# One kernel of cross attention and a state-space scan: block 0's sampled maxima spread on TensorE, a longer planned transfer for the other blocks, and a new table of dates

## The chip, the cores and the metric

The kernel runs on one core of one Trainium2 chip. Its time is the device time of one execution in microseconds (us); three timed runs of the kernel before gave a median of 1900.03 (1899.72 to 1900.69). The core's engines are named as in the profile: PE is TensorE (products), PEld its weight load, DVE VectorE, ACT ScalarE, POOL GpSimd, SP SyncE, which issues most DMA transfers; "ACTq" and "SPq" are the DMA issues in ACT's and SP's streams. Each engine runs its own instructions strictly in the order in which the program gave them.

## The reference

All is float32. 4096 queries (rows of x, 512 wide) attend to 3202 context rows, with 8 heads of 64:

```python
xq, kv = layernorm(x, g1, beta1), layernorm(ctx, g1, beta1)
x = x + mha(xq, kv)                      # softmax over 3202 keys, then W_o, b_o
xn = layernorm(x, g2, beta2)
U = (xn @ W_in.T + b_in) @ Bmat          # 64 wide
s = silu(s @ A.T) + u_t                  # a scan over the 1024 steps of each of 4 rows
out = x + s @ Cmat + (program_probs.mean(1) @ W_prog.T + b_prog)
```

## The kernel before

**Prologue.** `lead()` prepares the context: 26 chunks of at most 128 keys are loaded (cx), normalised (xh), transposed to channel-major ct (on PE, tile tp_c, or by DVE and DMA), and multiplied by the key and value weights wk and wv. Four chunks make a group. Group 0 is multiplied plainly (products pv and pk). Groups 1 to 5 use a scheme with seven products in place of eight (`seventh`, L503: pkx, pky, pvx, pvy); ACT copies the one half of a result (ks, vs), DVE joins the other (L699), and SP stores keys in kd and values in vd. The last group is chunk 24 and a chunk of two keys; the values of these two go through `second` (L728, ACT, and L729, DVE) into the tile vx, by four DMA stores (L734).

**Sample.** The exponents of a block of queries need an offset that is at least near the largest score. For each block of 512 queries, products of its queries with a sample of the keys (sm, L426) are copied by ACT to ex (L442, "held"); DVE takes their maximum m over each partition (L446); the maxima of all partitions have to reach all partitions, and go out to DRAM and come back broadcast (md<-m, L449, "sent"; all<-md, L453, "got", both on SP); DVE reduces these to the offsets `shifts` and to `marks` (L459 to L462, "base"); and ACT turns the sample's scores into weights (L467, "extra"), since two of the sampled columns are keys of the sequence that are in no chunk.

**Attention.** There are 8 blocks of queries, in units of two heads each; for each half chunk of keys, PE makes scores s (L1280), ACT weights p=exp(s) with the offset (L1324), DVE adds them in acc (L1332), and PE multiplies by the values into po (L1386, and L1375 for ex with vx). At the unit's end, ACT copies and DVE joins the two parts of acc (L1355, L1309, L1360) and of po (L1467, L1474). PE runs scores some groups ahead of products. The last block goes in halves; behind it the tail finishes the scan.

**What sets the order.** `Plan.order()` (L153) simulates the engines while the program is built, and appends to each engine, whenever it is free, the ready piece with the earliest due time. A piece has a cost, pieces that it comes after, rings (buffers) that it takes and gives back, and a due time to which `SHIFT[name] * STEP` (STEP is 2150 ns) is added; LATE adds a delay before another engine sees a result (`"SP": 5000` for a transfer). The costs and dates exist only in that simulation: they decide the order of instructions, not how long the chip takes. One plan makes the prologue (with `used(c)` and `start_of(g)` as base dates), another attention and tail. `sample_pieces` adds a block's sample to either.

Of the kernel before, what the change touches and what calls it, by code (L numbers as in the profile page):

```python
# [10 lines left out]
F32 = mybir.dt.float32  # L11
# [9 lines left out]
P = 128  # L21
TB = 32
NC = H // P
NCH = 26
CK = 128
NDC = NCH // 2
REST = S2 - (NCH - 1) * CK
GC = 4
# [48 lines left out]
class Plan:  # L77
# [19 lines left out]
        "a": 31.5, "add": 70, "add.h": 168, "add.l": -0.25, "added": 30.75, "b": 38, "base": 4.75,  # L97
        "close": -10.5, "copied": 80.5, "counted": 21.25, "den": -120, "den.l": -21, "differ": 46.5,
        "extra": -64.75, "fall": 325.25, "fall.h": 51.75, "fall.l": -4.25, "fold.h": -94.5, "fold.l": 17.5,
        "gather": -4, "gather.h": -20, "gather.l": 41.25, "got": 5.75, "held": 14.75, "inverse": 86.5,  # L100
        "inverse.h": -73.5, "inverse.l": 49.5, "join": -20.5, "join.h": -32, "join.l": 82.5, "joined0": 167.5,
        "joined1": 27.5, "l.copy": 36.25, "l.factors": 17, "l.from": 127, "l.h": 7.25, "l.idle": 354.5,
        "l.inputs": 16.75, "l.kept": -25, "l.mod": -54.75, "l.near": -48.25, "l.out": 23.5, "l.scaled": 24.25,
        "l.states": 141, "l.stats": 402.5, "l.terms": 43, "l.turn": 199.5, "l.x1": -10.25, "l.ys": -4.75,
        "l.z": -59.25, "last": 37.75, "maximum": -59.75, "number": 40.75, "open": 0.5, "output": -7.75,
        "output.h": -18.75, "output.l": -43.25, "outs": 1.5, "outs.read": -4.25, "product": -7.25,
        "products": 30, "py1": 17, "query.factors": 4.25, "query.flip": 381.5, "query.load": 1.25,
        "query.move0": -7.5, "query.move1": -39.25, "query.move2": -38, "query.move3": 29.25,
        "query.scaled": 130.75, "query.stats": 673.25, "rest": 5, "rest.h": -59.75, "rest.l": -51,
        "risen": 16, "row.copy": 25.25, "row.flip": 59.5, "row.kept": -28, "row.load": -73.75,  # L110
        "row.mod": -54.75, "row.move0": 78.75, "row.move1": -81.5, "row.move2": 26.75, "row.move3": 146.5,
        "row.scaled": 88, "row.stats": -20.75, "row.store": 190.5, "row.x1": -56, "rows.first": 8.5,
        "rows.inputs": 577.75, "rows.outs": -105.25, "rows.s": 38, "rows.turn": 3.75, "sample": -21.5,
        "scale": -90.5, "scale.h": -17, "scale.l": 4.5, "scores": -8.5, "sevenths": -324.5, "sq": -9.5,
        "start": -45.75, "states": -0.5, "stored0": -22.25, "sums": 5.75, "sums.h": -0.5, "sums.l": -4.25,
        "swap": 65.5, "swap.h": 3.5, "swap.l": -19.25, "table": 18.25, "to": 7.75, "tq": 62.75,
        "weights": 17.75, "yb": -25, "a.load": 176, "bu": 72.25, "c.copy": -73.25, "c.factors": 11,
        "c.flip": 129, "c.load": -50.5, "c.move": -3.75, "c.scaled": -1.25, "c.stats": 4.75, "c.turn": -10.75,
        "d.bi": -16, "d.bm": 249.75, "d.cb2": 54.75, "d.rows": -23.75, "d.win": 17.5, "d.wo": -2,
        "d.wq": -221.25, "d.x0": 18, "h0": -29.5, "in": -84, "in.bi": 1.75, "in.bm": 21.75, "in.cb": -16.25,  # L120
        "in.cb2": 119, "in.rows": -45.5, "in.win": 126, "in.wk": 56, "in.wo": 0.5, "in.wq": -58.25,
        "in.x0": -103.75, "k": 1.25, "k.copy": -57.25, "k.sample": -12, "keep": 2, "marks": -22, "mean": 49,
        "modb": 17.5, "p": 14, "pb": 35, "pm": 49.75, "prm": 257.75, "prr": 69.5, "pt": -50.5, "pw": -26.25,
        "rowb": 64.25, "rowv": -21.5, "rowv.w": 108.75, "s": 33.5, "store": -22.75, "sums_": 2.75,
        "t": 218.25, "tied": 2.75, "v": 123.25, "wct": -62.25, "wk": -19.5, "wk.bias": -1.5, "wk.g": -64.75,
        "wk.pb": -83, "wk.w": -61.5, "wq": 2.75, "wq.bias": -7.75, "wq.g": -6.25, "wq.pb": 56.75,
        "wq.w": 56.5, "wv": 139.25, "wv.bias": 87.25, "wv.pb": 120, "wv.w": 11.75, "x.copy": 4,
        "x.factors": 108.75, "x.scaled": -158.25, "x.turn": 13.5, "heads": 41.5, "q": -13.75,
# [119 lines left out]
def xattn_ssm_kernel(  # L248
# [22 lines left out]
    nc = tc.nc  # L271
# [136 lines left out]
    def sampled_by(Q):  # L408

        v = {}  # L410
# [53 lines left out]
        def extra():  # L464
# [3 lines left out]

        return (
            ("sample", "PE", 870, sample, ["m", "m"], []), ("held", "ACT", 1200, held, ["ex"] if Q else [], ["m"]),  # L470
            ("maximum", "DVE", 1100, maximum, ["max"], []), ("sent", "SP", 300, sent, [], []),
            ("got", "SP", 300, got, [], []), ("base", "DVE", 700, base, [], ["max"]),
            ("extra", "ACT", 1300, extra, [], []),
        )

    def sample_pieces(add, Q, after, d, of_q=()):

        name, before, opened = None, after, {}
        for i, (name, engine, cost, run, takes, gives) in enumerate(sampled_by(Q)):
            for ring in takes:  # L480
                opened[ring] = (name, Q)
# [2368 lines left out]
```

## Time and profile before

| what | value |
|---|---|
| median of three runs | 1900.03 us (1899.72 to 1900.69) |
| profiled execution, its span | 1901.1 us, 1899.3 us |
| mean granted TensorE clock | 0.993 |
| PE busy | 1861.1 us, 98% of the span |
| DVE, ACT, POOL busy | 1492.1 us (79%), 1141.3 us (60%), 305.6 us (16%) |
| PE busy in 0 to 200 us, 200 to 1830, 1830 to the end | 186.16 of 200, 1617.97 of 1630, 56.99 of 69.3 |

In the rows quoted below, a time line's row gives the start and the duration in us, the engine and line, the operation with its result and sources, and in brackets the idle time of the engine just before it and what ended that. "<-issue" means that the profile shows nothing that it waited for. A row of waits gives the total idle time, how often, and the longest. Durations of groups ("x16") run from the first to the last of consecutive like instructions.

### The profile page before, as it was taken

To read this page: it belongs to the slowest core of one execution; us is meant where nothing else is said; L and a number is where in the kernel's file an instruction comes from. 1 tells how busy PE (TensorE), PEld (TensorE's weight loads), DVE (VectorE), ACT (ScalarE), POOL (GpSimd) and SP (SyncE) were. 2 spreads that over 40 slices of the span, in tenths; PEclk is the share of its full clock that TensorE was granted. 3 is DMA by queue.
4 is the path that set the end of the run, shared out by engine and by line. 5 is a ranking of instruction groups with operands and counts; after the bars stand their busy time and mean duration, and the time that the engine had idled before them with its cause. 6 is when DMAs were issued, how large, how long until landed. Compare 5 with 4: busy or idle time off the path is not lost.

```text
span 1899.3 us, 44466 instructions
## 1 busy us (share of the span) xinstructions
PE 1861.1 (98%) x17952; PEld 920.0 (48%) x17952; DVE 1492.1 (79%) x1731; ACT 1141.3 (60%) x1407; POOL 305.6 (16%) x395
## 2 busy tenths in 40 slices
PE   8899999999999999999999999999999999999997
PEld 5788433434343343434343434334443434577674
DVE  6541488789887889688978887888978897888776
ACT  3332377565766657565757576775667575657653
POOL 5220121001210221022101220022102210111105
PEclk9999999999999999999999999999999999999999
DMA  6652322250434124331434043413432143435667
GB/s 230 165 160 83 88 77 70 57 148 29 126 92 126 51 75 126 107 87 39 124 76 135 28 125 89 133 44 99 115 102 80 47 126 89 150 108 153 179 183 240
DMA packets 262993, 207.05 MB, mean 109 GB/s; under 512 B 95918, under 2 KB 236222, under 8 KB 262784
## 3 DMA queue, kind: packets, MB, share of 16 engines
q1 hardware_dynamic: 258764, 197.54, 36.7%
q10 hardware_dynamic: 4020, 6.62, 1.2%
q8 instruction: 143, 2.34, 0.5%
q14 instruction: 66, 0.54, 0.1%
HBM read 157.37 MB, written 29.89 MB: 99 GB/s over the span
## 4 chain that ended last, share of the span: by engine, by line
PE 81%; DMA 3%; DVE 2%; ACT 2%; issue 1%; ACTq 0%; DVEq 0%; SPq 0%; POOLq 0%
PE s L1280 29%; PE po L1386 29%; PE po L1411 5%; PE s L1293 4%; PE qx L503 3%; PE pax L503 3%; PE pay L503 2%; PE qy L503 2%; DMA all<-md 2%; DMA md<-m 1%; ACT p L1324 1%; PE pd L1440 1%; DVE acc L1332 1%; PE pu L1900 1%; PE po L1375 1%
## 5 line engine op out<-in xcount | busy, mean ns | idle before, releaser
L1324 ACT ACTIVATE p<-s,shifts 128x1024 f32<-128x1024 f32 x804 | 888.2, 1109 | 412.1 <-PE s L1280 345.7
L1332 DVE TENSOR_TENSOR acc<-p,acc 128x1024 f32<-128x1024 f32 (+1 forms) x732 | 911.4, 1250 | 115.2 <-ACT p L1324 88.8
L1280 PE MATMUL s<-q,k 64*64 64x512 f32 x5600 | 724.2, 591 | 11.9 <-ACT p L1324 11.9
L1386 PE MATMUL po<-p,v 64*64 64x512 f32 x5600 | 722.3, 590 | 0.0
L1280 PEld LDWEIGHTS s<-q,k 64*64 64x64 f32 x5600 | 211.0, 133 | 401.3 <-issue 355.4
L1386 PEld LDWEIGHTS po<-p,v 64*64 64x64 f32 x5600 | 212.1, 133 | 355.9 <-issue 330.2
L1787 POOL TENSOR_TENSOR xr<-xr,rowb 128x512 f32<-128x512 f32 x28 | 35.4, 1273 | 701.1 <-DVE acc L1332 608.0
L1498 DVE RECIPROCAL rd<-rd 128x256 f32<-128x256 f32 (+1 forms) x64 | 110.2, 1721 | 27.5 <-ACT rd L1493 27.5
L1411 PE MATMUL po<-p,v 64*64 64x256 f32 x1600 | 112.2, 377 | 0.0
L1293 PE MATMUL s<-q,k 64*64 64x256 f32 x1600 | 112.1, 377 | 0.0
L1882 POOL TENSOR_TENSOR xr<-x,modb 128x512 f32<-128x512 f32 x28 | 35.3, 1269 | 279.9 <-DVE x L1835 265.7
L1293 PEld LDWEIGHTS s<-q,k 64*64 64x64 f32 x1600 | 67.3, 133 | 25.5 <-issue 3.8
L1411 PEld LDWEIGHTS po<-p,v 64*64 64x64 f32 x1600 | 67.2, 133 | 21.3 <-issue 1.7
L1568 POOL TENSOR_SCALAR rstd_x<-mv_x 128x1 f32<-128x1 f32 x28 | 30.6, 1093 | 279.5 <-DVE mv_x L1565 277.8
L1576 ACT ACTIVATE xh_y<-x,nm_y,rstd_y 128x512 f32<-128x512 f32 x30 | 24.2, 807 | 83.5 <-POOL nm_y L1570 83.5
L1332 DVE TENSOR_TENSOR acc<-p,p 128x1024 f32<-128x1024 f32 x36 | 44.6, 1239 | 27.5 <-ACT p L1324 27.3
L699 DVE TENSOR_TENSOR ks<-pky,ks 128x512 f32<-128x512 f32 x15 | 10.4, 690 | 49.7 <-PE pky L503 30.7
L1718 ACT ACTIVATE q<-qx,bias 128x256 f32<-128x256 f32 x42 | 17.6, 470 | 50.8 <-PE qx L503 50.8
L693 ACT ACTIVATE ks<-pkx,bias 128x256 f32<-128x256 f32 x40 | 16.7, 469 | 47.9 <-PE pkx L503 34.8
L1360 DVE TENSOR_TENSOR acc<-swap,acc 64x512 f32<-64x512 f32 (+1 forms) x70 | 44.1, 630 | 1.2
L1355 ACT COPY swap<-acc 64x512 f32<-64x512 f32 (+1 forms) x70 | 40.2, 574 | 2.0 <-DVE acc L1339 0.8
L598 DVE STREAM_TRANSPOSE x<-xh_x 128x512 f32<-128x512 f32 x28 | 19.6, 704 | 15.2 <-ACT xh_x L1576 10.7
(319 smaller groups left out, 1750.9 us busy)
## 6 DMA issues: line engine op xcount, KB each, us to landing
k<-kd SPq DMA_DIRECT2D x432, 128.0 KB, 2.6
v<-vd SPq DMA_DIRECT2D x432, 128.0 KB, 2.6
xn<-x SPq DMA_DIRECT2D x448, 32.0 KB, 1.9
xr<-in_x_dram SPq DMA_DIRECT2D x30, 256.0 KB, 4.2
x1d<-xr SPq DMA_DIRECT2D x30, 256.0 KB, 3.1
x<-in_x_dram SPq DMA_DIRECT2D x28, 256.0 KB, 4.0
cx<-in_ctx_dram SPq DMA_DIRECT2D x25, 256.0 KB, 3.8
vd<-vs SPq DMA_DIRECT2D x40, 128.0 KB, 2.1
```

The costliest lines, as they stand in the source:

```text
L503: nc.tensor.matmul(to[:, b, :], still[:, i, b * P : (b + 1) * P], moving[:, i, :], start=(start and b == 0 and i == 0), stop=(i == 1), ski ...
L1280: nc.tensor.matmul(s[k0 : k0 + HD, a].rearrange("p b j -> p (b j)"), kts[(*w["at"][:2], c // 2)][r, b * CK + k0 : b * CK + k0 + HD], q[r], ...
L1293: nc.tensor.matmul(s[k0 : k0 + HD, a, b, :], kts[(*w["at"][:2], c)][r, b * CK + k0 : b * CK + k0 + HD], q[r], start=True, stop=True, skip_ ...
L1324: nc.scalar.activation(t[:, :, :nb, :], w["ps"][c][:, :, :nb, :], AF.Exp, bias=w["shift"])
L1332: return nc.vector.tensor_tensor(w["acc"][:, :, :nb, :], t[:, :, :nb, :], before[:, :, :nb, :], ALU.add)
L1355: nc.scalar.copy(w["swap"][r], of[(1 - k) * HD : (2 - k) * HD])
L1360: made = nc.vector.tensor_tensor(of[r], w["swap"][r], of[r], ALU.add)
L1386: nc.tensor.matmul(w["po"][k][a * HD : (a + 1) * HD], vts[Q, hp, c // 2][r, c % 2, a * HD : (a + 1) * HD], t[r, a].rearrange("p b j -> p ( ...
L1411: nc.tensor.matmul(w["po"][k][a * HD : (a + 1) * HD, :QU], vts[Q, hp, c][r, b, a * HD : (a + 1) * HD], t[r, a, b, :], start=(c == 0 and b ...
L1498: nc.vector.reciprocal(w["rd"][:, part], (w["pd"] if last else w["rd"])[:, part])
L1787: return nc.gpsimd.tensor_tensor(xs[half][:, t], xs[half][:, t], rowb, ALU.add)
L1882: return nc.gpsimd.tensor_tensor(xt[:, t], x1[:, t], modb, ALU.add)
```

## The change

Four things are changed.

1. Block 0's maxima no longer go through DRAM. `spread` makes two PE products of 128x128 (a column of m, broadcast, times the identity) into a PSUM tile of the ring "m", and base reads that, with another arrangement of the same numbers. Block 0's names get the prefix "first.".
2. For the other blocks, a piece "landed" of cost 3000 on the planner's engine "IN" stands between got and base. It emits no instruction; the plan takes the transfer to be 3 us longer.
3. The last group's values are due 25000 ns later, its keys 8000 ns before the group's start instead of 5000 after it, block 0's sample 4000 instead of 14000 after it; and its ks has a tag of its own, "ks_l", outside the ring ks.
4. The table SHIFT is another one. Names of prologue pieces (c.*, d.*, in.*, wk.*, k, v, p, t, store and others) are no longer in it, and so are not moved; the values for attention and tail are other numbers.

```diff
     SHIFT = {
-        "a": 31.5, "add": 70, "add.h": 168, "add.l": -0.25, "added": 30.75, "b": 38, "base": 4.75,
...
-        "wq.w": 56.5, "wv": 139.25, "wv.bias": 87.25, "wv.pb": 120, "wv.w": 11.75, "x.copy": 4,
...
+        "a": -67, "add": -20, "add.h": -162.25, "add.l": 34, "added": 71.5, "b": -293.5, "base": -117.75,
...
+        def spread():
+            t = v["all"] = m_tile([P, 512], "spread")[:, : 2 * P]
+            for g in range(2):
+                nc.tensor.matmul(
+                    t[:, g * P : (g + 1) * P], v["m"][:, g : g + 1].to_broadcast([P, P]), ident,
+                    start=True, stop=True,
+                )
...
-            of = v["all"].rearrange("p (t b k g) -> p g b t k", t=2, b=2, g=2)
+            by = "p (t b k g) -> p g b t k" if Q else "p (g t b k) -> p g b t k"
+            of = v["all"].rearrange(by, t=2, b=2, g=2)
...
+        over = (("sent", "SP", 300, sent, [], []), ("got", "SP", 300, got, [], [])) if Q else (
+            ("spread", "PE", 500, spread, ["m"], []),
+        )
...
+            if name == "got":
+                add((sort + "landed", Q), "IN", 3000, lambda: None, before, d + 1000 * i)
+                before = [(sort + "landed", Q)]
...
-            v, u = {}, used(c)
+            v, u = {}, used(c) + (25000 if c >= n_g * GC else 0)
...
-            u, v = start_of(g) + (14500 if g == 0 else 5000) + hp * (3560 if g == 0 else 1000), {}
+            u, v = start_of(g) + (14500 if g == 0 else -8000) + hp * (3560 if g == 0 else 1000), {}
...
+                if g:
+                    v["ks"] = cin.tile([P, CK + REST], F32, tag="ks_l", name=f"ks_{g}_{hp}", bufs=NC)
...
-                      start_of(n_g) + 14000)
+                      start_of(n_g) + 4000, sort="first.")
```

The order of the instructions at four places follows, before and after. Numbers at the end of a name tell tiles of one kind apart and differ between the two programs.

PE at the start: turns of chunks (tp_c) and value products of group 0 (pv), before and then after.

```order
L1215 MATMUL idle<-a_t 128x128 x11
L362 MATMUL tp_c_189<-ident,xh_c_185 128x128 x4
L362 MATMUL tp_c_223<-ident,xh_c_220 128x128 x4
L362 MATMUL tp_c_230<-ident,xh_c_217 128x128 x4
L716 MATMUL pv_238<-wv,ct_188 128x512 x4
L716 MATMUL pv_250<-wv,ct_188 128x512 x4
```

```order
L1221 MATMUL idle<-a_t 128x128 x11
L351 MATMUL tp_c_189<-ident,xh_c_185 128x128 x4
L719 MATMUL pv_223<-wv,ct_188 128x512 x4
L351 MATMUL tp_c_234<-ident,xh_c_220 128x128 x4
L351 MATMUL tp_c_241<-ident,xh_c_217 128x128 x4
L719 MATMUL pv_253<-wv,ct_188 128x512 x4
```

The first value product has moved ahead of the second and third turn.

ACT about 50 us in: copies ks of the key products, normalisations xh_c, and loads that ACT issues (cb, rowb, modb, wp_t, a_t), before and then after.

```order
L853 ACTIVATE ks_3_570<-pk_3_535,bias 128x512
L1004 DMA cb<-in_ctxb_2048x_dram 128x1600
L346 ACTIVATE xh_c_585<-cx_338,nmr_c_562,rstd_c_560 128x512
L1004 DMA cb_595<-in_ctxb_2048x_dram 2x64
L693 ACTIVATE ks_11_597<-pkx_564,bias 128x256 x2
L1026 DMA rowb<-in_L_xattn_b_o_dram 128x512
L1027 DMA modb<-in_L_xattn_b_prog_dram 128x512
L1028 DMA wp_t<-in_L_xattn_W_prog_dram 64x512
L1030 DMA a_t<-in_L_xattn_A_dram 64x64 x2
L693 ACTIVATE ks_12_643<-pkx_564,bias 128x256 x2
```

```order
L1010 DMA cb<-in_ctxb_2048x_dram 128x1600
L1010 DMA cb_494<-in_ctxb_2048x_dram 2x64
L335 ACTIVATE xh_c_512<-cx_232,nmr_c_453,rstd_c_451 128x512
L650 COPY ct_315<-tp_c_514 128x4x128
L335 ACTIVATE xh_c_535<-cx_280,nmr_c_478,rstd_c_476 128x512
L696 ACTIVATE ks_11_551<-pkx_523,bias 128x256 x2
L692 COPY vs_11_578<-pvx_537 128x512
L335 ACTIVATE xh_c_599<-cx_293,nmr_c_509,rstd_c_507 128x512
L335 ACTIVATE xh_c_603<-cx_390,nmr_c_549,rstd_c_547 128x512
L335 ACTIVATE xh_c_615<-cx_429,nmr_c_576,rstd_c_574 128x512
L1032 DMA rowb<-in_L_xattn_b_o_dram 128x512
```

The copies ks_11 and vs_11 now stand between the loads of cb and those from rowb on, which are followed by ks_12 as before.

PE from block 0's last sampled product to the third group of scores, before and then after (pky, pvx, pvy are products of group 5, pb, prr and prm small row products, pv those of the last group).

```order
L426 MATMUL sm_1_1556<-q_2_1538,kx 32x256
L503 MATMUL pky_1482<-ct_1232,sk_524 128x256 x4
L503 MATMUL pvx_1474<-wv,t_5_1349 128x256 x4
L503 MATMUL pvy_1489<-sv_381,ct_1232 128x256 x4
L979 MATMUL pb_1603<-ones,shift_wv 128x1 x4
L716 MATMUL pv_1609<-wv,ct_1398 128x512 x4
L716 MATMUL pv_1628<-wv,ct_1398 2x512 x4
L1107 MATMUL prr<-shift_rowv,ones 128x512
L1107 MATMUL prm<-wp_t,mean 128x512
L1280 MATMUL s_0_0_0_1691<-q_0_1430,k_0_0_0_510 64x512 x4
L1280 MATMUL s_0_0_1_1696<-q_0_1430,k_0_0_0_510 64x512 x4
L1280 MATMUL s_0_0_2_1709<-q_0_1430,k_0_0_1_518 64x512 x4
```

```order
L415 MATMUL sm_1_1595<-q_2_1537,kx 32x256
L719 MATMUL pv_1615<-wv,ct_1448 128x512 x4
L447 MATMUL spread<-ident,m_1623 128x128 x2
L719 MATMUL pv_1628<-wv,ct_1448 2x512 x4
L1286 MATMUL s_0_0_0_1691<-q_0_1493,k_0_0_0_386 64x512 x4
L1286 MATMUL s_0_0_1_1696<-q_0_1493,k_0_0_0_386 64x512 x4
L1286 MATMUL s_0_0_2_1709<-q_0_1493,k_0_0_1_398 64x512 x4
```

Six groups of products have moved ahead of the sample. On ACT, the copies at this place (before: extra, second, then the copy vs of chunk 24) now stand in the order extra, vs of chunk 24, second, and then the first weights, as before.

ACT at the end of block 0, where block 1's sample lies (p are weights of the last unit of block 0, rd the reading of an earlier unit's sums), before and then after.

```order
L1324 ACTIVATE p_3_0_10_3127<-s_3_0_10_3113,shifts 128x1024
L467 ACTIVATE ex_3048<-ex_3048,marks 128x2x256 x2
L1324 ACTIVATE p_3_0_11_3141<-s_3_0_11_3129,shifts 128x1024
L1324 ACTIVATE p_3_0_12_3156<-s_3_0_12_3147,shifts 128x1024
```

```order
L1330 ACTIVATE p_3_0_11_3141<-s_3_0_11_3129,shifts 128x1024
L1499 ACTIVATE rd_2_0_3147,rises<-pd_2_0_0_3135 128x256
L1499 ACTIVATE rd_2_0_3147,rises<-pd_2_0_1_3136 128x256
L1330 ACTIVATE p_3_0_12_3164<-s_3_0_12_3153,shifts 128x1024
L465 ACTIVATE ex_3059<-ex_3059,marks 128x2x256 x2
L1330 ACTIVATE p_3_0_13_3182<-s_3_0_13_3170,shifts 128x1024
```

The extra now comes behind the twelfth weights instead of the tenth. On DVE, the base of block 1 comes behind the eleventh addition of that unit instead of the eighth.

More of the change, by code (lines that the diff above doesn't have):

```diff
@@ L102 @@
[L102 to L122, printed above, removed]
@@ new lines @@
+        "got": 26.5, "held": 47.75, "inverse": 341.5, "inverse.h": 1.5, "inverse.l": -3.75, "join": -16,
+        "join.h": -387.25, "join.l": -15.25, "joined0": -53, "joined1": 63.25, "l.copy": -152.75,
+        "l.factors": 126, "l.from": 9, "l.h": 14.5, "l.idle": 259.75, "l.inputs": 113.5, "l.kept": -43.5,
+        "l.mod": -344.25, "l.out": 1, "l.scaled": 106, "l.states": 10.75, "l.stats": 52.25, "l.store": 71.5,
+        "l.terms": 29.5, "l.turn": 25, "l.x1": 21.75, "l.ys": 2.75, "l.z": -1, "landed": -6.25, "last": -354,
@@ new lines @@
+        "row.move2": 183, "row.move3": 63.75, "row.row": 46, "row.scaled": -89.75, "row.stats": 34.5,
+        "row.store": 21.5, "row.x1": -80, "rows.inputs": 32.5, "rows.s": -1, "rows.turn": 0.75,
+        "sample": -640.5, "scale": 41, "scale.h": 74.75, "scale.l": -84.5, "scores": -1, "sent": 55.75,
+        "sevenths.read": -56.5, "so": -69, "sq": -2.5, "start": 56.25, "states": 3.5, "stored0": -60,
+        "stored1": -32.25, "sums": -6.75, "sums.h": -161.25, "swap": 14.5, "swap.h": 2, "swap.l": -94.25,
```

47 lines of the change are left out of this document (24 added, 23 removed).

## The prediction

> **What bounds the kernel now.** I read the cores' line first, then the page's busy times, the waits of PE, the table by stage, and the time line of each stage where PE stood still. One profiled execution took 1901.1 us, with a span of 1899.3, so 1.8 us lie outside the span; the median of the three timed runs is 1900.03, 1.07 under the profiled one. The sums below are made against 1901.1 and shifted by 1.07 at the end.
>
> ```profile
> core 0: 1899.3 us, clock 0.993
> PE 1861.1 (98%) x17952; PEld 920.0 (48%) x17952; DVE 1492.1 (79%) x1731; ACT 1141.3 (60%) x1407; POOL 305.6 (16%) x395
> PE s L1280 <- ACT p L1324: 11.9, 8, 4.5
> PE pkx L503 <- ACT ks L693: 7.2, 2, 5.9
> PE tp_c L362 <- DVE xh_c L631: 3.7, 2, 3.5
> ```
>
> PE is the bound. Its idle time is 1899.3 − 1861.1 = 38.2 us, and the change neither adds nor removes a product worth counting, so only that idle time and slow-clock time can move. The three wait rows (total, times, longest) hold 22.8 of it. The scores' row is one wait of 4.5 and seven that share 11.9 − 4.5 = 7.4, one at each of the seven block boundaries (I found them in the time line with 0.6 to 1.4 each).
>
> ```profile
> 10.00:25.00 15.00, 14.10 (x36) 7.04 (x37) 5.92 (x16) 5.88 (x9) 8.01 (x21) 0.81 0.58 178
> 50.00:70.00 20.00, 14.12 (x59) 9.88 (x59) 9.96 (x21) 5.30 (x10) 7.08 (x15) 0.83 0.59 156
> 110.00:190.00 80.00, 80.00 (x407) 67.92 (x407) 23.05 (x47) 27.48 (x52) 7.03 (x22) 1.00 0.38 109
> 190.00:235.00 45.00, 40.48 (x234) 19.74 (x236) 18.61 (x24) 17.31 (x23) 6.95 (x4) 0.92 0.31 88
> ```
>
> Columns: stretch, sum, busy time of PE, PEld, DVE, ACT, POOL, granted clock, DMA share, GB/s. Where PE idles long, the clock falls too: busy time times the missing clock is 14.10 × 0.19 = 2.7, 14.12 × 0.17 = 2.4 and 40.48 × 0.08 = 3.2 us. From 110 to 190 there is nothing to win. So the change is worth what it does at five places.
>
> **A, the start.** These are the rows of the first 25 us.
>
> ```profile
> 6.13 0.77 PE L362 MATMUL tp_c<-ident,xh_c 128*128 128x128 f32 x4 [0.20 <-DVE xh_c L631]
> 6.93 0.65 ACT L647 COPY ct<-tp_c 128x256 f32<-128x256 f32 x2 [3.69 <-PE tp_c L362]
> 9.55 0.45 DVE L583 TENSOR_SCALAR wv<-raw_v,g1s 128x512 f32<-128x512 f32 x1
> 10.39 1.12 PE L362 MATMUL tp_c<-ident,xh_c 128*128 128x128 f32 x4 [3.49 <-DVE xh_c L631]
> 12.92 8.40 PE L716 MATMUL pv<-wv,ct 128*128 128x512 f32 x16
> 21.16 0.60 PE L362 MATMUL tp_c<-ident,xh_c 128*128 128x128 f32 x4
> 21.60 3.60 PE L716 MATMUL pv<-wv,ct 128*128 128x512 f32 x8
> ```
>
> PE turns chunk 0, waits 3.49 for chunk 1, turns the next two chunks and only then makes the value products of chunks 0 and 1, at a low clock (8.40 for sixteen passes, where eight take 3.60). The change puts the first of them into that hole, straight behind the first turn. What it needs is there: chunk 0's copy ends at 6.93 + 0.65 = 7.6, and the last piece of wv at 9.55 + 0.45 = 10.0, ahead of the eight-pass group's last quarter. At full clock it runs 7.7 to 11.3; two turns of 0.6 make 12.5, the next product 3.6 more: 16.1, where before it was 12.92 + 8.40 = 21.3. Gain 5.2. If the clock is as low as the 8.40 says (4.2 for each product, 1.12 for each turn) the same chain ends at 7.7 + 4.2 + 2.2 + 4.2 = 18.3: gain 3.0. Later starvation by DMA could take some more, so bounds 3 to 6; I take 5.2, since the hole that let the clock fall is what gets filled.
>
> **B, the key copy behind the queue.**
>
> ```profile
> 50.03 1.89 PE L503 MATMUL pky<-ct,wk 128*128 128x256 f32 x8
> 56.23 0.51 ACTq L1004 DMA_DIRECT2D cb<-in_ctxb_2048x_dram  x1
> 56.86 0.47 ACT L693 ACTIVATE ks<-pkx,bias 128x256 f32<-128x256 f32 x1 [6.53 <-DMA cb<-in_ctxb_2048x_dram]
> 57.79 3.75 PE L503 MATMUL pkx<-t,sk 128*128 128x256 f32 x8 [5.88 <-ACT ks L693]
> ```
>
> ACT stood 6.53 us at the issue of the load of cb, with the copy of the product pkx right behind it in its stream; PE's next pkx needs that copy's ring place and waited 5.88, then ran at half speed (3.75 against 1.89). In the new order the copies ks and vs of that pair stand ahead of the next blocking issues, and the cb issues stand six rows earlier, with three normalisations and a turn's copy between. Taken away whole: 5.88 + (3.75 − 1.89) = 7.7. The later issues (rowb, modb, wp_t, a_t) still stand ahead of the second pair's ks, so some waiting may reappear there; bounds 0 to 7.7, taken 7.0, because the copy that was waited for is past all of them.
>
> **C, two short waits at 100 us.**
>
> ```profile
> 101.27 1.99 PE L503 MATMUL pkx<-t,wk 128*128 128x256 f32 x8 [1.28 <-ACT ks L693]
> 104.53 1.78 PE L503 MATMUL pky<-ct,sk 128*128 128x256 f32 x7 [1.27 <-DVE ks L699]
> ```
>
> Together 2.6. New dates spread these copies; but the groups' transposed chunks come by DMA with 1 to 3 us to spare by my reading of the order, so bounds −3 (a loss) to +2.6, taken +1.5.
>
> **D, the way into attention.** T is the start of block 0's last sampled product, 201.51 before.
>
> ```profile
> 201.51 1.09 PE L426 MATMUL sm<-q,kx 64*32 64x256 f32 x32
> 203.79 1.22 DVE L446 TENSOR_REDUCE m<-ex 128x2 f32<-128x1024 f32 x1 [6.03 <-ACT ex L442]
> 208.62 5.49 PE L716 MATMUL pv<-wv,ct 128*128 128x512 f32 x16
> 212.12 0.48 DVE L459 TENSOR_REDUCE shifts<-all 128x2 f32<-128x128 f32 x2 [1.06 <-DMA all<-md]
> 214.58 0.58 ACT L728 COPY second<-pv 2x512 f32<-2x512 f32 x1
> 215.19 0.68 DVE L729 TENSOR_TENSOR second<-pv,second 2x512 f32<-2x512 f32 x1 [1.40 <-ACT second L728]
> 215.93 2.84 SPq L734 DMA_DIRECT2D vx<-second  x4
> 216.16 1.95 PE L1280 MATMUL s<-q,k 64*64 64x512 f32 x16
> 221.45 2.12 ACT L1324 ACTIVATE p<-s,shifts 128x1024 f32<-128x1024 f32 x2 [5.69 <-issue]
> 222.62 1.98 PE L1280 MATMUL s<-q,k 64*64 64x512 f32 x8 [4.52 <-ACT p L1324]
> ```
>
> The round trip of the maxima (m at 203.79 to shifts at 212.12) looks like the thing removed, and is worth nothing here: the first weights start at 221.45, 8.8 us after the shifts, with "issue" for a cause. What came last is the transfer of vx out of `second`, whose SBUF the weights take over: join end 215.87 to p_0 is 5.58. Before, eight groups of products lay between sample and scores and covered most of that. In the new order six of them lie ahead of the sample, and only the value products of the last chunk and of the two keys over it, and `spread` (two 128x128 products, 0.3 us by half of a four-part turn's 0.60) follow it.
>
> Step by step: the sampled product 1.0, chunk 24's value product 3.6, to T + 4.6. Maximum, as before, ends at 203.79 + 1.22 − 201.51 = T + 3.5; spread to T + 4.9; the base, 1.0, to T + 5.9; ACT's extra 1.3, copy of chunk 24 0.6 and `second` 0.6, one behind another, to T + 8.6; the join 0.7, T + 9.3. PE had ended its products at T + 6.7 (5.49 for both, less 3.6, is 1.9 for the short one). The first scores take the PSUM place that the join reads, so PE idles 2.6 to 2.7; two groups of scores run to T + 11.1. The weights, 5.58 behind the join, start at T + 14.9, and the third scores 1.17 later (222.62 − 221.45), T + 16.05. Idle 2.7 + 4.9 = 7.6 against 4.52, and some 0.4 of clock: **a loss of 3.5**. Bounds: 1 (if the store's wait is shorter once SP has fewer transfers ahead) to 6 (if the clock halves over the whole of it, as the pkx row of B shows). The last group's earlier keys, later values and own `ks_l` tile cost nothing beyond this: the same products are in a stage that the table shows full, 110 to 190.
>
> By the Trainium skill ("TensorE: Matmul & The Clock Gate", "Why this matters for your kernels") gaps over about 3 us are to be avoided, since one window of idling halves the rate. The trace agrees in kind: 3.49 and 5.88 have slow rows behind them, the short gaps at the block boundaries none. By it the 2.7 gap would cost its length and no clock; if not, the two score groups after it would cost about 2 us more, within the bound of 6.
>
> **E, seven block boundaries.** This is the one at 371 to 387 us.
>
> ```profile
> 375.77 0.32 SPq L449 DMA_DIRECT2D md<-m  x1
> 379.12 0.32 SPq L453 DMA_DIRECT2D all<-md  x1
> 379.55 1.22 DVE L1332 TENSOR_TENSOR acc<-p,acc 128x1024 f32<-128x1024 f32 x1 [0.49 <-ACT p L1324]
> 383.58 0.48 DVE L459 TENSOR_REDUCE shifts<-all 128x2 f32<-128x128 f32 x2 [2.81 <-DMA all<-md]
> 384.67 1.33 ACT L467 ACTIVATE ex<-ex,marks 128x512 f32<-128x512 f32 x2 [1.73 <-DVE marks L462]
> 387.06 1.09 PE L1280 MATMUL s<-q,k 64*64 64x512 f32 x8 [1.06 <-ACT p L1324]
> ```
>
> The planner reckoned the transfer short by 2.81 us: DVE stood at the base, ACT at `extra` for 1.73, and the weights behind `extra` came late by 1.73 plus its 1.33, less the slack. The reserve moves the base behind three more additions (3 × 1.22 = 3.7, more than 2.81) and `extra` two weights later. The two transfers end at 383.6, 11.7 us after the sample; in the new order base ends near 14 after the sample, `extra` starts as the weights before it end, and the weights after it are late by its own 1.33 less ACT's slack of 0.60 between weights: about 1.0 with what the copies before took, under the 1.3 that PE's two groups ahead cover. So all seven gaps go: −7.0 of 7.4. Bounds 3 to 7.4, for boundaries where another of ACT's tasks lies in the same place (there the 1.0 becomes a gap of up to 0.6 each, 4.2 in all).
>
> **F, the tail:** its first steps come slightly earlier in the order; nothing there waits on what moved. 0, bounds −1 to +1.5.
>
> **Sum:** 5.2 + 7.0 + 1.5 − 3.5 + 7.0 = 17.2 us; 1901.1 − 17.2 = 1883.9 by the profile, 1882.8 by the median: **1883 us**. The bounds of B to E do not all fall one way; the forecast's own range is 1878 to 1888.
>
> **Rivals.** *R1, the queue's wait only moves.* ACT is held at a later issue instead, and B brings 1 rather than 7, C loses 1 instead of gaining 1.5: 1883 + 6 + 2.5 = 1891. For it: the waiting was in the queue, and there are as many issues as before. Against: the copy that PE needs is no longer behind them. *R2, the reserve does nothing.* It names no instruction; if the transfer lands later in step with it, or the gap comes from `extra` itself, E is 0: 1883 + 7 = 1890. Against it stands the row with 2.81: DVE was at the base before the data were. By the Trainium skill ("DMA: Bandwidth & Descriptors", "Anatomy of one DMA — SWDGE (gpsimd) path") a transfer has about 2.0 us of fixed cost; two would be about 4, and the old reserve was enough, which gives the same 1890 by an estimate from that page. The trace says 3.35 from the one issue to the next and 4.5 to the reduction, and so speaks against it. *R3, slower: the unit changes break.* Scores run one group less ahead of the products in the new order, and at a unit's change the new products wait for DVE's join of the old sums:
>
> ```profile
> 418.06 0.68 DVE L1474 TENSOR_TENSOR o<-po,o 128x512 f32<-128x512 f32 x1
> 418.88 1.90 PE L1386 MATMUL po<-p,v 64*64 64x512 f32 x16
> ```
>
> The join ends at 418.74 and the products start 0.14 later. One more addition (1.22) ahead of the join would stall PE by 1.22 − 0.14 = 1.08 at each of the 28 changes after block 0's: 30 us, 1883 + 30 = 1913. It decides from 17.2 / 28 = 0.6 us a change. Against it: my count of the new order has the join in time by about 0.1, no better than before but no worse.
>
> **How the numbers follow.** Forecast 0.65, R1 0.15, R2 0.12, R3 0.08. The range reaches to the rivals on the near side: 1877 to 1892. A measurement of this kernel tells 0.2%, 3.8 us, from no change, so faster means under 1896.2. Forecast, R1 and R2 are all faster alone; where R1 and R2 fall together with D at its worst, about 1895 to 1898, the time is the same: faster 0.86, same 0.06, slower 0.08.
>
> **What would show it.** Right: no hole over 1 us between 7 and 16 us; no 5.88 before pkx near 50 us, and the first weights near 211 instead of 221; two idle times of PE before attention's third score group of about 2.7 and 4.9, with p named "issue" again; `shifts` at the seven boundaries without a wait for a DMA and no gap before scores there. Wrong: slow clock in 0 to 25 us unchanged (A), a new wait of PE on ACT behind rowb or a_t (R1), boundary gaps still there with ACT busy (R2), or PE waiting for `o` on DVE 28 times (R3).

## The result, and the profile after

The changed kernel takes 1880.31 us (median of four runs, 1878.88 to 1880.37), the kernel before 1900.1 beside it: a ratio of 0.9894, 95% interval 0.9877 to 0.9911, so 17 to 23 us are gone. 1883 was forecast, 1877 to 1892 allowed. The profiled execution took 1878.88 with a span of 1877.1; against the profiled 1901.1 before that is 22.2 us, and the account below is made between these two traces.

The cores' line and the page's busy times of the changed kernel (its source lines are numbered 11 lower than before up to the sample, and 3 to 6 higher behind it):

```profile
core 0: 1877.1 us, clock 0.997
PE 1856.2 (99%) x17956; PEld 921.5 (49%) x17956; DVE 1485.5 (79%) x1731; ACT 1143.2 (61%) x1407; POOL 291.9 (16%) x395
```

Its two largest waits of PE, total, times and longest:

```profile
PE s L1286 <- ACT p L1330: 2.9, 1, 2.9
PE s L1286 <- DVE second L732: 2.5, 1, 2.5
```

And three stages, with the columns of the table shown before:

```profile
10.00:25.00 15.00, 14.32 (x46) 7.05 (x46) 12.71 (x21) 6.12 (x10) 12.11 (x14) 1.00 0.84 257
50.00:70.00 20.00, 20.00 (x108) 17.05 (x105) 11.67 (x25) 4.28 (x9) 3.16 (x9) 1.00 0.70 190
185.00:225.00 40.00, 34.65 (x242) 14.88 (x245) 16.31 (x17) 17.62 (x22) 7.51 (x7) 0.91 0.30 88
```

PE's idle time fell from 38.2 to 20.9 us. The wait of a product on the copy ks has left the list, and so has the turn's long wait. The scores' wait on the weights, 11.9 us eight times, is one wait of 2.9, with a new one of 2.5 on `second` beside it: both lie at the way into attention. The clock is full in the two stages of the prologue where it had been 0.81 and 0.83.

The start of the time line of PE, and the way into attention:

```profile
6.08 0.76 PE L351 MATMUL tp_c<-ident,xh_c 128*128 128x128 f32 x4 [0.45 <-DVE xh_c L634]
7.30 3.76 PE L719 MATMUL pv<-wv,ct 128*128 128x512 f32 x8 [0.46 <-ACT ct L650]
12.38 7.04 PE L719 MATMUL pv<-wv,ct 128*128 128x512 f32 x16
...
193.19 1.09 PE L415 MATMUL sm<-q,kx 64*32 64x256 f32 x32
198.40 0.49 DVE L457 TENSOR_REDUCE shifts<-spread 128x2 f32<-128x128 f32 x2 [1.70 <-PE spread L447]
201.94 0.68 DVE L732 TENSOR_TENSOR second<-pv,second 2x512 f32<-2x512 f32 x1 [2.53 <-ACT second L731]
202.67 3.64 PE L1286 MATMUL s<-q,k 64*64 64x512 f32 x16 [2.49 <-DVE second L732]
202.68 2.82 SPq L737 DMA_DIRECT2D vx<-second  x4
205.61 0.38 SPq L829 DMA_DIRECT2D vd<-vs  x1
208.00 2.12 ACT L1330 ACTIVATE p<-s,shifts 128x1024 f32<-128x1024 f32 x2 [6.09 <-DMA vd<-vs]
209.17 1.62 PE L1286 MATMUL s<-q,k 64*64 64x512 f32 x8 [2.85 <-ACT p L1330]
```

The first value product fills the hole at a full clock; the second ends near 12.4 + 3.5 = 15.9. In attention's start the offsets are there at 198.9, and the weights start at 208.0. What they wait for has a name this time: the store of chunk 24 (vd<-vs), which stands behind the four stores of `second` on SP.

The first block boundary:

```profile
363.07 0.32 SPq L438 DMA_DIRECT2D md<-m  x1
366.13 0.32 SPq L442 DMA_DIRECT2D all<-md  x1
372.64 0.47 DVE L457 TENSOR_REDUCE shifts<-all 128x2 f32<-128x128 f32 x2
373.73 1.33 ACT L465 ACTIVATE ex<-ex,marks 128x512 f32<-128x512 f32 x2
```

Neither the reduction nor the extra has a wait in brackets any more, and no gap of PE stands behind them.

Where the 22.2 us came from: third scores of block 0 start at 209.17 instead of 222.62, which is 13.45 of the span; the other 8.75 come behind it, 7.4 of them the seven gaps. The 13.45 split at the sample (193.19 after, 201.51 before). Six groups of products, 8.2 us by their starts in the trace before, now lie ahead of the sample, so up to the sample 201.51 + 8.2 − 193.19 = 16.5 are won; and from sample to third scores 15.98 pass instead of 21.11 − 8.2 = 12.9, which is 3.1 lost. The 1.35 of the 8.75 that are not in the gaps are answered under F below.

### The profile page after: what moved, and what is told of

Its sections match the earlier page's. It is cut to its first block, busy times and chain, and to the rows that moved or that the text cites. A ratio compares the mean times of both kernels' runs of the same rounds, so it can differ in the third digit from the quotient of the medians.

```text
span 1877.1 us, 44496 instructions
## 1 busy us (share of the span) xinstructions
PE 1856.2 (99%) x17956; PEld 921.5 (49%) x17956; DVE 1485.5 (79%) x1731; ACT 1143.2 (61%) x1407; POOL 291.9 (16%) x395
## 4 chain that ended last, share of the span: by engine, by line
PE 97%; DMA 1%; DVE 0%; ACT 0%; POOL 0%; issue 0%; SPq 0%; ACTq 0%; POOLq 0%; DVEq 0%
PE po L1392 32%; PE s L1286 32%; PE po L1417 5%; PE s L1299 5%; PE pax L506 3%; PE qx L506 3%; PE pay L506 2%; PE qy L506 2%; PE pkx L506 2%; PE pvx L506 2%; PE pvy L506 1%; PE pky L506 1%; PE pk L846 1%; PE pv L719 1%; PE pq L381 1%; PE pd L1446 1%
## 5 line engine op out<-in xcount | busy, mean ns | idle before, releaser
L1299 PE MATMUL s<-q,k 64*64 64x256 f32 x1600 | 108.1, 377 | 0.0
L1417 PE MATMUL po<-p,v 64*64 64x256 f32 x1600 | 107.5, 377 | 0.0
L1299 PEld LDWEIGHTS s<-q,k 64*64 64x64 f32 x1600 | 64.4, 133 | 25.1 <-issue 3.4
L1417 PEld LDWEIGHTS po<-p,v 64*64 64x64 f32 x1600 | 65.1, 133 | 20.9 <-DMA xn<-x 0.8
L1574 POOL TENSOR_SCALAR rstd_x<-mv_x 128x1 f32<-128x1 f32 x28 | 18.0, 644 | 212.5 <-DVE mv_x L1571 210.7
L435 DVE TENSOR_REDUCE m<-ex 128x2 f32<-128x1024 f32 x8 | 9.8, 1220 | 37.2 <-ACT ex L431 37.2
```

The costliest lines, as they stand in the source:

```text
L1299: nc.tensor.matmul(s[k0 : k0 + HD, a, b, :], kts[(*w["at"][:2], c)][r, b * CK + k0 : b * CK + k0 + HD], q[r], start=True, stop=True, skip_ ...
L1417: nc.tensor.matmul(w["po"][k][a * HD : (a + 1) * HD, :QU], vts[Q, hp, c][r, b, a * HD : (a + 1) * HD], t[r, a, b, :], start=(c == 0 and b ...
```

## The experiments

The runs were made in three groups of four. The kernel before, run beside each of them, took 1896.6 and 1898.6 us with the first two, both recorded as chip 9, and 1898.7 with the third, on chip 13. Each run is compared with the kernel before of its own group; times in us that follow are the ratio times 1898, and a bracket behind one is its 95% interval. Where an experiment moves pieces, it does so by hand in the list that the planner returns, with this helper:

```diff
-        for piece in plan.order():
+        ordered = plan.order()
+        named = {p["name"]: p for p in ordered}
+
+        def put(name, behind, other):
+            p = named[name]
+            ordered.remove(p)
+            ordered.insert(ordered.index(named[other]) + behind, p)
```

### One part alone, in the kernel before

**The first value product.**

```diff
+        put(('v', 0), 0, ('c.turn', 1))
```

> The kernel before, with one move on PE: the first value product goes ahead of the second and third turn, as in the change; every other engine's order is as before. Theory (term A of the prediction): the 3.49 us hole is filled and the clock stays up, the second product ends near 16 instead of 21.3 us, and PE, which has little slack after that, keeps it: 3 to 5.2 us faster, 1895 to 1897. Rival: what waits later (the key copy behind the blocked issue at 50 to 56 us) takes it back, because that wait ends with a transfer and not with PE: 0 to 1 us faster.

Measured: 1890.11 against 1896.62, ratio 0.9963 (0.995 to 0.9977): 7.0 us faster (4.4 to 9.5), by the median more than the 5.2 of the sum, which the interval includes. Its time line of PE:

```profile
7.69 4.02 PE L716 MATMUL pv<-wv,ct 128*128 128x512 f32 x8 [0.97 <-DVE wv L583]
...
52.60 3.46 PE L503 MATMUL pkx<-t,sk 128*128 128x256 f32 x8 [5.38 <-ACT ks L693]
...
216.14 1.98 PE L1289 MATMUL s<-q,k 64*64 64x512 f32 x8 [4.37 <-ACT p L1333]
```

The later wait is still there, but 5.2 us earlier (57.79 before): it moved with PE, so the rival falls. Third scores come 6.5 earlier than in the trace before. At the start itself 4.7 are won: the third value product starts at 16.91 instead of 21.60. The other 1.8 come at the later wait, which is shorter (5.38 for 5.88) and has a shorter slow stretch behind it: the slow product takes 3.46 for 3.75, the next one 1.94 for 2.90.

**The key copy ahead of a blocked issue.**

```diff
+        put('d.cb2', 1, ('keep', 1, 0, '11'))
```

> The kernel before, with one move on ACT: the issue of the two-row load of cb goes behind the key copy ks that stood behind it; nothing else moves. Theory (term B): PE's 5.88 us wait and the slow pkx behind it (1.86 us) go: 6 to 7.7 us faster, about 1893. Rival R1 (the waiting only moves on to the next issue and the next copy behind it): 0 to 1.5 us faster.

Measured: 1894.81, ratio 0.9989 (0.998 to 0.9998): 2.1 us faster (0.4 to 3.8). That is far under the theory's 6 to 7.7; the rival's 0 to 1.5 lies within the interval, though under the median. The wait of 5.88 is gone from the time line, and 19 us later there is this, on ACT, SP, DVE and PE:

```profile
59.24 2.75 ACTq L1030 DMA_DIRECT2D a_t<-in_L_xattn_A_dram  x2
62.12 0.84 ACT L693 ACTIVATE ks<-pkx,bias 128x256 f32<-128x256 f32 x2 [10.76 <-DMA modb<-in_L_xattn_b_prog_dram]
69.15 2.44 SPq L617 DMA_DIRECT2D cx<-in_ctx_dram  x4
75.41 0.69 DVE L325 BATCH_NORM_STATS2 st_c<-cx 128x6 f32<-128x512 f32 x1 [7.93 <-DMA cx<-in_ctx_dram]
76.31 0.66 DVE L699 TENSOR_TENSOR vs<-pvy,vs 128x512 f32<-128x512 f32 x1
77.11 3.65 PE L503 MATMUL pvy<-sv,ct 128*128 128x256 f32 x8 [4.57 <-DVE vs L699]
```

Read it from the bottom: PE waits 4.57 for a join; the join stands on DVE behind statistics that waited 7.93 for a chunk; the chunk's load was issued at 69; and ACT, whose normalisations free the buffers of such loads, had stood for 10.76 us at its own issues up to 62. With the slow product behind it (3.65 for 1.89) this costs 6.3 of the 7.7 won; third scores start at 220.93, 1.7 earlier than before.

**The same, with the other issues moved away too.**

```diff
+        put('d.cb2', 1, ('keep', 1, 0, '11'))
+        put('d.rows', 1, ('keep', 4, 0, '11'))
```

> The kernel before with the move of key_copy_alone, and with the issues of rowb, modb, wp_t and a_t moved on ACT from there to a quiet place, behind a key copy of group 4; nothing else moves. Theory (why B alone brought only 2 us): ACT stood at those issues until 62 us, so the normalisations, the chunk loads that wait for their buffers, and the statistics on DVE with the join behind them came late, and PE lost at 77 us what it had won at 58. With both moved, 6 to 8 us faster than before. Rival: the loads are late because transfers are full at that time, whatever ACT does: 1 to 3 us faster, as with the copy alone.

Measured: 1894.35 against 1898.66, ratio 0.998 (0.9971 to 0.9989): 3.8 us faster (2.1 to 5.5), under the theory's range; by the median it is over the rival's 1 to 3, into which the interval reaches. The waits at 58 and 77 us are gone from this trace and the next one appears:

```profile
94.52 3.66 PE L503 MATMUL pkx<-t,wk 128*128 128x256 f32 x8 [2.88 <-ACT ks L693]
...
217.12 1.60 PE L1290 MATMUL s<-q,k 64*64 64x512 f32 x8 [4.61 <-ACT p L1334]
```

Third scores stand 5.5 us ahead of the trace before, where the copy alone had 1.7. By these traces ACT's blocked issues were a part of the cause, then; the intervals of the two times overlap, and the two runs were on different chips. That transfers are full there may be another part: no run tries it, and what is left isn't divided.

**The reserve.**

```diff
+            if name == "got" and Q:
+                add(("landed", Q), "IN", 3000, lambda: None, before, d + 1000 * i)
+                before = [("landed", Q)]
```

> The kernel before with the planner's 3 us reserve and nothing else of the change: on each of the seven boundaries the base stands two additions later on DVE and the extra one weight later on ACT; PE's, SP's and the prologue's orders are as before. Theory (term E): DVE no longer stands at the base, the seven gaps of together 7.4 us shrink to 0.1 or so each: 6 to 7.4 us faster, about 1893. Rival R2 (the reserve does nothing, the gap comes from the extra itself): within 1 us of before.

Measured: 1891.97, ratio 0.9974 (0.9963 to 0.9984): 4.9 us faster (3.0 to 7.0), by the median under the theory's 6 to 7.4. The waits of PE by cause show that the mechanism did all that was expected, with one wait of the scores left, the one at 222 us:

```profile
PE s L1283 <- ACT p L1327: 4.3, 1, 4.3
```

There was less to win in the traces of this group. In that of the key copy alone, whose order at the seven boundaries is that of the kernel before, the scores' row reads

```profile
PE s L1289 <- ACT p L1333: 8.5, 8, 4.2
```

that is 8.5 − 4.2 = 4.3 us in seven gaps, where the profile before had 7.4. The same boundaries in the old order lost 3.6 in the trace of the first value product and 2.8 in that of the spread below, both on chip 9, and 6.6 in that of the key copy and rows, on chip 13. With one trace of each, a chip can't be told from an execution here. DVE waited 16.9 or 17.3 us in eight for these transfers in two of the traces of this group, against 20.7 in the profile before.

**The spread.** The piece "sent" of block 0 does nothing, "got" runs `spread`, and the base reads PSUM; everything keeps its place.

```diff
+            ("sent", "SP", 300, sent if Q else (lambda: None), [], []),
+            ("got", "SP", 300, got if Q else spread, [], []),
```

> The kernel before, with block 0's maxima spread by two products in place of the two transfers; the base and all else stay where they were in order. Theory (term D): the first weights wait for the stores out of `second` and not for the maxima, so the time is the same within 1 us (0.5 faster at most, since the extra ahead of `second` on ACT can start earlier). Rival: the round trip set the start of attention, and its removal takes PE's 4.5 us wait away: 1895.5.

Measured: 1895.51, ratio 0.9996 (0.9987 to 1.0005): no difference. The maxima are spread at 205, the weights start where they did:

```profile
205.10 0.61 PE L458 MATMUL spread<-ident,m 128*128 128x128 f32 x4
210.43 0.48 DVE L468 TENSOR_REDUCE shifts<-spread 128x2 f32<-128x128 f32 x2
220.30 2.12 ACT L1333 ACTIVATE p<-s,shifts 128x1024 f32<-128x1024 f32 x2 [5.49 <-DMA vd<-vs]
```

### The prologue's dates, and the moves together

**The new dates for the prologue alone.** In the kernel before, `plan.SHIFT = {}` for the prologue's plan, which gives it the change's dates; transfers, reserve, the last group's dates and attention's table stay as before.

> The kernel before with the change's dates for the prologue alone (no entry of the table applies there); transfers of the maxima, the last group's own dates and attention as before. The planner then puts both value products of the last group ahead of the sample, and only the scores behind it. Theory: the prologue's gains as in the change's trace (16.5 us to the sample, work moved counted), but now nothing covers the round trip: offsets 10.6 us after the sample, third scores 14.2 after it where the same work before took 7.5: 6.7 lost, the seven gaps kept, 8 to 12 us faster than before. Rival: the round trip costs nothing here either, 15 to 17 faster.

Measured: 1891.73, ratio 0.9956 (0.9943 to 0.997): 8.4 us faster, as expected. Up to the sample this trace wins 14.0 (16.5 in the change; 1.35 of the difference is a wait at 125 us), but third scores come only 7.6 earlier, so 6.4 are lost again behind it. The reason stands in its time line: with the value products ahead of the sample nothing covers the round trip. DVE's `shifts` waits 7.87 for `all`, ACT's weights for DVE, and PE for the weights

```profile
213.82 1.11 ACT L1325 ACTIVATE p<-s,shifts 128x1024 f32<-128x1024 f32 x1 [9.84 <-DVE marks L462]
214.99 1.98 PE L1281 MATMUL s<-q,k 64*64 64x512 f32 x8 [9.01 <-ACT p L1325]
```

So the spread, worth nothing alone, takes away a wait that these dates lay bare. The change also moves block 0's sample and the last group's dates; no run has the change without the spread, so what the spread alone is worth in it isn't measured.

**The old dates for the prologue, in the change.** `plan.SHIFT` of the prologue's plan is the old table; the rest is the change.

> The changed kernel with the old table for the prologue's plan alone; spread, reserve, the last group's dates and the new dates of attention stay. Theory: A, B and C are given back (13 to 16 us), what is left is E less D: 2 to 8 us faster than before. Rival: the prologue's dates are worth little and the gain sits in attention: 14 or more faster than before.

Measured: 1892.08, ratio 0.996 (0.9946 to 0.9974): 7.6 us faster than before, so 10 to 12 of the change's 17 to 20 are given back.

**Four moves by hand.** The kernel before with the first value product, the two moves on ACT and the reserve; no spread, no new dates.

> The kernel before with the first value product first, the two moves on ACT of key_copy_and_rows, and the reserve; no new dates, no spread. Theory: the places are apart on PE's line, so the gains add: 7 + 7 + 5, 16 to 20 us faster than before, no slower than the change. Rival: the prologue is paced by transfers, and the first value's gain and the key copy's are the same time: 12 to 14 us faster.

Measured: 1884.11, ratio 0.9921 (0.9908 to 0.9935): 15.0 us faster (12.3 to 17.5). By the median that is 1.0 under the theory's range and as much over the rival's 12 to 14, and the interval reaches into both. Alone the moves measured 7.0, 3.8 and 4.9, together 15.7, which fits gains that add, but doesn't exclude the rival. Third scores start at 214.61, 5.4 behind the change, and the largest wait that is left ahead of them is this one, which with its slow product is 3.35 + 1.86 = 5.2:

```profile
69.80 3.75 PE L506 MATMUL pvy<-sv,ct 128*128 128x256 f32 x8 [3.35 <-DVE vs L702]
```

### Steps undone or bettered in the change

**The change once more,** on the chip of the next three.

> The changed kernel itself, beside the next three on the same chip: every theory expects what was measured, 19 to 20 us under the kernel before, less what this chip's transfers are quicker by at the seven boundaries (on the chip of the first four runs some 3 us).

Measured: 1879.77 against 1898.56, ratio 0.9909 (0.9896 to 0.9923): 17.3 us.

**Without the reserve.**

```diff
-                add((sort + "landed", Q), "IN", 3000, lambda: None, before, d + 1000 * i)
+                add((sort + "landed", Q), "IN", 0, lambda: None, before, d + 1000 * i)
```

> The change with a reserve of 0 in place of 3000 ns; all but the base and the extra at the seven boundaries stays in order: the base stands two additions earlier on DVE, the extra ahead of the eleventh weights and of the reading of the sums on ACT. Theory (term E): the maxima are back 11.7 us after the sample, the base then ends 12.7 after it, the extra and one reading of sums make the next weights 3.6 us late where 1.3 are covered: a gap of about 2.3 at each boundary, 10 to 16 us slower than the change. Rival R2: the reserve does nothing, within 1 us of the change.

Measured: 1891.43, ratio 0.9961 (0.9948 to 0.9975), 11.7 us over the change by the medians. The first boundary:

```profile
366.14 0.32 SPq L442 DMA_DIRECT2D all<-md  x1
371.11 0.48 DVE L457 TENSOR_REDUCE shifts<-all 128x2 f32<-128x128 f32 x2 [1.81 <-DMA all<-md]
372.20 1.33 ACT L465 ACTIVATE ex<-ex,marks 128x512 f32<-128x512 f32 x2 [2.44 <-DVE marks L460]
374.95 1.09 PE L1286 MATMUL s<-q,k 64*64 64x512 f32 x8 [1.71 <-ACT p L1330]
```

In full view: data 1.81 late, ACT held 2.44, PE 1.71. The reserve is worth more in the new order than in the old one, probably because the weights there stand earlier behind the sample, which no run tries apart: p_3_0_10 9.10 us after it (368.63 and 359.53 in the changed kernel), 9.96 before (381.83 and 371.87).

**`second` ahead of the sample.**

```diff
+        put(('v', 25), 0, ('p', 5, 1, '3'))
+        put(('v.copy', 25), 1, ('h0.q', 3))
+        put(('v.copy', 24), 0, ('first.extra', 0))
+        put(('v.store', 24), 1, ('v.copy', 24))
```

> The change, with the value product of the last two keys and its copy, join and stores (`second` to vx) ahead of block 0's sample, and the copy and store of chunk 24 ahead of the extra on ACT. Theory (term D): the first weights wait for the last store out of the SBUF that they take over; that store is now issued near T + 5.4 and not T + 12.4 (T is the sample's start, 1.8 later than in the change), lands 2.4 later, so the weights start near T + 8 instead of T + 14.8: 4 to 5 us faster than the change. Rival: the weights wait for the extra and the base, or the clock falls for longer: within 1 us of the change.

Measured: 1872.57, ratio 0.9864 (0.9849 to 0.9879); by the medians 7.2 us under the change, a version that beats both. Its way into attention:

```profile
197.19 1.09 PE L415 MATMUL sm<-q,kx 64*32 64x256 f32 x32
202.56 0.38 SPq L829 DMA_DIRECT2D vd<-vs  x1
202.59 1.95 PE L1298 MATMUL s<-q,k 64*64 64x512 f32 x16 [0.23 <-ACT vs L826]
204.95 2.12 ACT L1342 ACTIVATE p<-s,shifts 128x1024 f32<-128x1024 f32 x2
206.11 1.09 PE L1298 MATMUL s<-q,k 64*64 64x512 f32 x8 [1.58 <-ACT p L1342]
```

The weights start 7.8 after the sample (near 8 was expected, 14.8 in the change); two idle times of together 5.3 us are down to 1.8, and the scores run at 1.95 where they took 3.64. Third scores start 3.06 earlier than in the change (206.11 and 209.17). The next 24 score and 16 weighted-sum products then take 4.35 us instead of 6.04 (PE is at the scores of 210.46 here, of 215.21 in the change), because the clock is full: 1.00 from 185 to 225 us, where the change had 0.91. That is another 1.69. The sample itself comes 4.0 later than in the change, not the expected 1.8, since a wait ahead of it is new:

```profile
125.31 1.97 PE L506 MATMUL pkx<-ct,wk 128*128 128x256 f32 x8 [1.81 <-issue]
```

The spans of the two profiled executions differ by 5.1 (1877.1 and 1872.0), the medians by 7.2. Without that wait the spans would be about 6.9 apart, an estimate; whether the unprofiled executions had it isn't on record.

**The join late.** For each of the 28 unit changes before the last block, DVE's join stands behind the next addition:

```diff
+        for p in [p for p in ordered if p["name"][0] == "join" and p["name"][1] < Plan.HALVES]:
+            i = ordered.index(p)
+            k = next(k for k in range(i + 1, len(ordered)) if ordered[k]["name"][0] == "add")
+            ordered.remove(p)
+            ordered.insert(k, p)
```

> The change, with DVE's join of the old sums behind one more addition at each of the 28 unit changes before the last block; nothing else moves. Theory (R3's price): the join has 0.14 us to spare, so the products start 1.22 - 0.14 = 1.08 late at each, and PE has nothing else there: 30 us slower than the change. Rival: PE's scores ahead cover most of it, under 10 us slower.

Measured: 1904.86, ratio 1.0031 (1.0019 to 1.0043), 25.1 us over the change by the medians: 0.90 for each change of unit, as an average.

```profile
PE po L1392 <- DVE o L1480: 7.9, 12, 1.0
```

The page counts only 12 of these waits; PE's busy time is 15 us up at the same number of products, so the rest probably lies inside durations whose ends are modelled.

## Why the prediction was right

**A, the start, taken 5.2: mechanism right, and size right at its place.** The clock stayed up and the second product ended at 15.9 where 16.1 was worked out and 21.3 stood before, which is 5.4; alone the step won 4.7 there. That it measured 7.0 alone (4.4 to 9.5) comes from 35 us later, where the wait on the key copy and the slow stretch behind it were together 1.8 shorter. The sum has no term for that; it is luck as far as A goes.

**B, taken 7.0: right as a part of the change, wrong as a step by itself.** The wait and the slow product left the trace. But "the copy that was waited for is past all of them" named one victim of ACT's queue and left out the normalisations behind the same issues: what that sentence called its own 7.7 is 2.1 when the copy alone is moved and 3.8 with the issues gone too. The change has neither that wait nor one at the places where the moves by hand still wait (77 and 95 us). That its dates do this by starting the whole chain of loads, statistics and copies earlier is an argument; no run takes the dates apart.

**C, taken 1.5:** both waits are gone, 2.6; the feared loss from the transposed chunks isn't in the change's trace. It is in others with the same dates: the product on a transposed chunk at 125 us waits 1.35 in the run of the new dates alone, 1.81 with `second` early and 2.24 with the join late, all within the bound of 3 that C gave it. A to C together were 13.7 in the sum and 16.5 in the trace. The difference is not one wait: in the first 200 us PE's busy time went from 186.16 to 197.20, and the clock from 0.97 to 1.00.

**D, taken −3.5: right in kind and nearly in size.** With T the start of the sample, worked out were the weights at T + 14.9 and third scores at T + 16.05; they came at 14.81 and 15.98, a loss of 3.1. The spread alone measures as nothing, and early stores bring the weights 7 us nearer to the sample: the start of attention hung on stores. The store has another name than in the prediction: not the last one of `second`, but that of chunk 24 (vd<-vs), as it already was in the trace of the spread alone. SP issues it right behind the four of `second`, which is why the sum came out.

One part was mis-shared: the two idle times were 2.49 and 2.85 rather than 2.7 and 4.9, because the clock did fall, and the two score groups between took 3.64 instead of 1.95. The Trainium skill ("TensorE: Matmul & The Clock Gate", "Why this matters for your kernels") asks for no idle gap of PE over about 3 us, a limit that a gap of 2.49 us keeps. Here half rate followed such a gap all the same, in the change (2.49) and with the join late (2.50), while full-rate products followed gaps of 1.58, 1.71 and 2.24. Just ahead of both of the longer gaps PE has products with only two rows of output, so the gap by itself isn't shown to be the cause. Up to the third scores the half rate cost nothing, since PE was waiting for the weights anyway; behind them it went on, and the same work that takes 6.04 us there took 4.35 with `second` early.

**E, taken 7.0:** seven gaps of 7.4 gone in the trace. Done alone it is 4.9, beside traces whose seven gaps were 2.8 to 4.3; left out of the change it costs 11.7. R2 falls, and with it the estimate of some 4 us for both transfers from the Trainium skill ("DMA: Bandwidth & Descriptors", "Anatomy of one DMA — SWDGE (gpsimd) path"): in the trace without the reserve the first takes 3.06 to the second's issue, the second 4.97 more. That section is on transfers that GpSimd issues; these two stand in SP's queue.

**F, taken 0:** behind the third scores 1.35 us more are gone than the seven gaps explain, within the bound of 1.5 that F gave. The traces place them: 0.6 lie directly behind the third scores (6.04 us where the same work took 6.65 before), and 0.7 in the tail, which is 51.9 us from the start of the last attention product to the end of the span instead of 52.6.

**R1** is what happened to B alone, and not to the change. **R3** did not happen: PE doesn't wait for the join. Its price, 25.1 for 30, was right within a fifth, but in part by luck. The 0.14 us that it gives the join to spare was read from one change of unit; in the changed kernel the spare time is 0.13 to 0.18 at eight of them and some us at others, where PE has other work first. One of each kind:

```profile
401.85 0.68 DVE L1480 TENSOR_TENSOR o<-po,o 128x512 f32<-128x512 f32 x1
402.67 1.90 PE L1392 MATMUL po<-p,v 64*64 64x512 f32 x16
449.27 0.68 DVE L1480 TENSOR_TENSOR o<-po,o 128x512 f32<-128x512 f32 x1
458.84 1.95 PE L1392 MATMUL po<-p,v 64*64 64x512 f32 x16
```

With the join late, the loss differs from change to change as well (0.36 to 1.72 us), because the next addition stands at another distance each time; 0.90 is the mean of unlike ones.

So 17.2 was forecast, 22.2 is in the traces and 19.8 between the medians; most of what missed was in the prologue (16.5 for 13.7), where each wait was priced singly, and the rest is D's 0.4, E's 0.4 and F's 1.35.

## What to carry to other kernels

A wait in a prologue full of transfers is rarely one wait: before pricing its removal, list everything that stands behind the same blocked issue, and look 20 us on for what is late next. A planned reserve should be the measured time from the send to the first use, and the slack of the order around it decides what a microsecond too little costs. Where a stage starts with buffers taken over from the stage before, look for the last store that reads them; bringing that store forward was worth more here than removing a round trip that was already covered.

## What was not expected of the hardware

Behind a gap of PE of 2.49 us the granted clock was 0.50 (204 to 206 us, two score groups in 3.64 us); behind gaps of 1.58 to 2.24 the products ran at full rate. The time that the same transfers take differs between executions by enough to matter: the seven gaps, in the same order of work there, lost 7.4 us in the profile before and 2.8 to 6.6 in later traces; whether the chip or the execution makes the difference is open. And on ACT an issue held up the engine for 6.5 us, and a run of issues for 10.8, though each is 0.4 to 0.7 us of work.
